# Last image of a four-layer convolution network: six pieces of the output stage loaded ahead, into the tiles of the finished scans

## The chip, the cores and the metric

The kernel runs on one core of a Trainium2 chip. The metric is the device time of one execution in microseconds (us). The core has a tensor engine (TensorE, matmuls, results in PSUM), a vector engine (VectorE), a scalar engine (ScalarE), GpSimd, and SyncE (SP), whose queue issues nearly all DMA transfers here. The engines run their own instruction streams and wait for each other by semaphores. A profile takes one execution apart.

## The reference

Four layers run one after the other on a tensor of 4 images with 64 channels of 128 x 128. The first three (attention with a spectral gate, Fourier mixing with experts, a Hartley layer with a Gaussian blur) are untouched. The change lies in the last one, which sums two state-space scans and its input:

```python
ys = mamba_fwd(xs, ...)                      # one sequence over all images and pixels
spa = silu(group_norm(ys, gn_w, gn_b, 4)) + x
ye = mamba_fwd(xe, ...)                      # short sequences over groups of channels
spe = x + silu(group_norm(ye, ...))
w = softmax(att_w)
return spa * w[0] + spe * w[1] + x
```

The group norm needs mean and variance of a whole image, so an image's output can only be finished once its scan has ended. Layer 2 masks the columns 33 to 95 of every row to zero, up to the blur's edges, so only 69 (`CW`) or 65 (`KW`) of the 128 columns of x are kept; in the masked columns the output is one constant per channel.

## The kernel before

Layer 3 (`layer3`) splits the work of the scans into units. The last 76 units (19, `SPC`, for each image) belong to the spatial scan: 483 positions each, 170 in an image's last one. A unit has 8 steps, one for each `q` in `ORDER` (0, 2, 4, 6, 1, 3, 5, 7). A step q makes `dA` on ScalarE (`do_exp`, L1472), `dB` on VectorE or GpSimd (`do_dB`, L1488), scans `h` from both on VectorE (`do_scan`, L1493), and multiplies `h` by C on GpSimd (`do_hc`, L1520). TensorE sums the products (`do_sums`); then come `do_y` (L1545) and `spa_out`, which brings the result to SBUF and stores it to the array `y1` in HBM (L1564). The states are eight tiles `hs` (h0 to h7, L1267) and eight tiles `dBs` (dB0 to dB7, L1279), each of 128 partitions x 1024 numbers. Both live to the end of the kernel.

When an image's last unit is through, `affine` (L1688) forms scale and shift of the two norms (`bn_aggr` on VectorE, small matmuls, a square root on ScalarE) and fills the constant columns of the output tiles (L1726). Then `combine` makes the image in eight pieces; piece i holds the rows 8i to 8i+7 in partitions 0 to 63 and the rows 64+8i to 64+8i+7 in partitions 64 to 127. Its parts are:

- part 0: six loads on SP's queue, three for each half of the partitions: f from `y1` (L1747), x from `x2s` (L1748), e from `ye` (L1749), of 138, 138 and 130 KB;
- part 1: SiLU with the norm's scale and shift on ScalarE, of f (L1752) and of e (L1753);
- parts 2 and 4: for half a piece each, the weighted sum of x, f and e as four matmuls with scaled unit matrices into PSUM (`ps_m`, two buffers);
- parts 3 and 5: VectorE copies the sum into the output tile (L1765, two copies for each half), and part 5 issues two stores of 256 KB (L1768).

`parts` gives the tiles f, x, e and out of a piece. They lie one behind the other in one of two buffers `big2`, so piece i shares its buffer with pieces i-2 and i+2, and piece i's loads wait until piece i-2 has been computed.

The order of the instructions on TensorE, VectorE, ScalarE and GpSimd is written out by hand: `scans` gives each call a due time in steps and emits the calls sorted by it. SP's queue is not in that list: the framework's scheduler orders it, and it moves DMAs that are free to go ahead of others. Each DMA on that queue uses one of eight semaphores in turn, and so also waits for the eighth DMA before it. For the first three images the pieces are spread between the units of the next image; for the last image there is nothing after them.

Of the kernel before, what the change touches and what calls it, by code (L numbers as in the profile page):

```python
# [17 lines left out]
NB, C, N = 4, 64, 128  # L18
# [6 lines left out]
ZC = 33  # L25
# [286 lines left out]
class Net:  # L312
# [1303 lines left out]
    def scans(self, us):  # L1616
        nc = self.nc
        self.turn, self.o1s = 0, {}
        chunks = GPX // CPX

        todo = []
        steps = [(u, q) for u in us for q in ORDER]
        by_pool = lambda j: ORDER[j % 8] not in BY_DVE
        for ci, u in enumerate(us):
            do = lambda when, f, *a: todo.append((8 * ci + when, len(todo), f, a))
            spa = u["spa"]
            if spa:
                do(-22.0, self.spa_load, u)
            else:
                for part, when in enumerate((-2.9, 4.7, 6.42)):  # L1630
                    do(when, self.do_first, u, part)
                m, i = divmod(u["at"], 4)
                do(-13.0, self.spe_taps, u)
                for g in range(8 if i == 0 else 0):

                    do(-48.0 + 3 * g if m > 1 else -48.0, self.spe_load, m, g)
                for g in range(8 if i == 3 or u["at"] == chunks - 1 else 0):
                    do(12.3 + 3 * g, self.spe_store, m, g)
            do(-12.9, self.do_x, u)
            for part, when in enumerate((-11.65, -11.25, -10.65, -10.05, -9.8, -9.55, -9.3, -9.0, -8.05)):  # L1640
                do(when, self.do_dt, u, part)
            do(-7.7, self.do_put, u, "dt")
            do(-7.4, self.do_put, u, "dx")
            for k, when in enumerate((-9.07, -8.85, -7.24, -6.59)):
                do(when, self.do_bc, u, k)
                do(when + 0.59, self.do_keep, u, k)
            for i, when in enumerate((4.7, 4.74, 5.9, 9.42, 9.74) if u["kind"] != "run" else ()):
                do(when, self.do_sums, u, i)
            if u["kind"] != "run":
                do(10.76, self.do_y, u)  # L1650
                do(12.2, self.spa_out if spa else self.spe_out, u)
                do(13.64, self.do_stats, u)
        mine = [j for j in range(len(steps)) if not by_pool(j)]
        for j, (u, q) in enumerate(steps):
            do = lambda when, f, *a: todo.append((j + when, len(todo), f, a))
            do(-6.0, self.do_copy, u, q, "dt")
            do(-1.56, self.do_exp, u, q, 0)
            do(-1.2, self.do_exp, u, q, 1)
            if by_pool(j):
                do(-6.5, self.do_copy, u, q, "dx")  # L1660
                do(-4.22, self.do_dB, u, q, nc.gpsimd)
            else:
                do(-1.61, self.do_dB, u, q, nc.vector)
            do(0.1, self.do_scan, u, q, 0)
            do(0.5, self.do_scan, u, q, 1)
            if u["kind"] == "run":
                do(0.55, self.keep_run, u, q)
            else:
                do(0.77, self.do_hc, u, q)
        for k, j in enumerate(mine):  # L1670

            when = mine[k - 1] - 1.28 if k else -2.0
            todo.append((when, len(todo), self.do_sel, steps[j]))
        for ci, u in enumerate(us):
            if u["kind"] == "spa" and u["at"][1] == SPC - 1:
                b = u["at"][0]
                do = lambda when, f, *a: todo.append((8 * ci + when, len(todo), f, a))
                do(15.8, self.affine, b)
                for i in range(8):

                    for part, when in enumerate((4.0, 10.37, 16.3, 16.75, 16.8, 17.51)):
                        do(when + 8 * (i + 1), self.combine, b, i, part)
        E = mybir.EngineType
        with self.tc.manual_schedule(engines={E.PE, E.DVE, E.Activation, E.Pool}):
            for _, _, f, a in sorted(todo, key=lambda x: x[:2]):
                f(*a)

    def affine(self, b):  # L1688

        nc, c3, sm = self.nc, self.c3, self.small  # L1690
        mv = sm.tile([128, 2], F32, name="mv0")
        nc.vector.bn_aggr(mv, self.st0.rearrange("p k s -> p (k s)"))
        s0, t0 = self.norm_affine(sm, mv, c3["gm16w"], c3["spa_gn_w"], c3["spa_gn_b"], self.eps)
        mv = sm.tile([128, 4, 2], F32, name="mv1")
        for g in range(4):
            nc.vector.bn_aggr(mv[:, g, :], self.st1[:, g].rearrange("p k s -> p (k s)"))
        gm = c3["gme"][:, 128 * b : 128 * b + 128]
        four = lambda name: sm.tile([128, 4], F32, name=name)
        p = self.ps("m")
        self.mm(p[:, 0:4], gm, mv[:, :, 0])  # L1700
        mean, q, rs = four("mean4"), four("q4"), four("rs4")
        nc.vector.tensor_copy(mean, p[:, 0:4])
        nc.vector.tensor_tensor(q, mv[:, :, 0], mean, ALU.subtract)
        nc.vector.tensor_tensor(q, q, q, ALU.mult)
        nc.vector.tensor_tensor(q, q, mv[:, :, 1], ALU.add)
        p = self.ps("m")
        self.mm(p[:, 0:4], gm, q)
        nc.scalar.activation(rs, p[:, 0:4], AF.Sqrt, bias=self.eps)
        nc.vector.reciprocal(rs, rs)
        one = lambda name: sm.tile([128, 1], F32, name=name)  # L1710
        s1, t1, m = one("s1"), one("t1"), one("m1")
        for of, to in ((rs, s1), (mean, m)):
            nc.vector.tensor_tensor(of, of, c3["goh"], ALU.mult)
            nc.vector.tensor_reduce(to, of, AX.X, ALU.add)
        nc.vector.tensor_tensor(s1, s1, c3["spe_gn_w"], ALU.mult)
        nc.vector.tensor_tensor(m, m, s1, ALU.mult)
        nc.vector.tensor_tensor(t1, c3["spe_gn_b"], m, ALU.subtract)
        self.st = (s0, t0, s1, t1)

        k0, k1 = one("k0"), one("k1")  # L1720
        nc.scalar.activation(k0, t0, AF.Silu)
        nc.scalar.activation(k1, t1, AF.Silu)
        nc.vector.tensor_tensor(k0, k0, c3["att"][:, 0:1], ALU.mult)
        nc.vector.scalar_tensor_tensor(k1, k1, c3["att"][:, 1:2], k0, ALU.mult, ALU.add)
        for i in range(2):
            nc.vector.tensor_copy(self.parts(i)[3][:, :, ZC:96], k1.unsqueeze(2).to_broadcast([128, 8, 96 - ZC]))  # L1726

    def parts(self, i):

        ws, at, out = (CW, CW, KW, N), 0, []  # L1730
        for w in ws:
            out.append(self.big2[i % 2][:, at : at + 8 * w].rearrange("p (h w) -> p h w", h=8))
            at += 8 * w
        return out

    def combine(self, b, i, part):

        nc, c3 = self.nc, self.c3
        R = 8
        f, x, e, out = self.parts(i)  # L1740
        flat = lambda t: t.rearrange("p h w -> p (h w)")
        sides = ((0, 0, 0, ZC), (ZC, ZC + 4, 96, KW - ZC))
        if part == 0:
            for hh in range(2):
                rows = slice(64 * hh, 64 * hh + 64)
# [8 lines left out]
        elif part in (2, 4):  # L1754
            p = self.three = self.ps("m")[:, : 4 * CW]
            at = slice(2 * part - 4, 2 * part)
            self.mm(p, c3["by_x"], flat(x[:, at]), stop=False)
            self.mm(p, c3["by_0"], flat(f[:, at]), start=False, stop=False)
            p = p.rearrange("p (h w) -> p h w", h=4)
            for j, (of, mid, to, w) in enumerate(sides):  # L1760
                self.mm(p[:, :, mid : mid + w], c3["by_1"], e[:, at, of : of + w], False, j == 1)
        else:
            p = self.three.rearrange("p (h w) -> p h w", h=4)
# [35 lines left out]
```

## Time and profile before

| | us |
|---|---|
| time, median of 3 runs | 7353.47 (7347.41 to 7354.81) |
| profiled execution | 7342.41 |
| its span | 7340.7 |
| last y store issued (L1564) | 7277.78 |
| norms known, first SiLU of the last image's output | 7287.74 |
| first store of its piece 0 / piece 4 | 7293.59 / 7318.42 |
| last copy of piece 7 (L1765) | 7335.34 |

Times in the lower rows are from the span's start. In the profile, lines name engine, line of the kernel, tile, and counts; "A" is a tile in one of the buffers `big2` (or a load tile of the scans), `h` and `dB` are the scans' tiles. A wait line names the waiting instruction, then what it waited for. In the chain of work that ended last, a line "DMA A<-ye" is the time from a load's issue until it has landed, and SPq is SP's queue.

### The profile page before, as it was taken

Reading aid. Unit: us, or ns where it says so; the run is one execution under the profiler, and the core shown is the slowest. Engines: PE = TensorE matmul, PEld = TensorE weight load, DVE = VectorE, ACT = ScalarE, POOL = GpSimd, SP = SyncE. Lnnn points to the kernel's source line nnn. Section 1 sums busy time; section 2 is a strip of 40 time slices with the busy share of each in tenths; the row PEclk is TensorE's granted clock in tenths of the full one; section 3 lists DMA queues with packets and bytes.
Section 4 is the critical chain, followed back from the end, with each engine's and each line's share of the span. In section 5 each row is a group of like instructions: output and inputs, shape, how many; then the busy total and the mean of one; then the engine's idle time right before and its main releaser. Section 6 shows DMA issues by size and latency. Waiting matters only on the chain.

```text
span 7340.7 us, 106844 instructions
## 1 busy us (share of the span) xinstructions
PE 6632.5 (90%) x39058; PEld 2873.7 (39%) x39058; DVE 5408.6 (74%) x7737; ACT 4771.6 (65%) x7768; POOL 3607.2 (49%) x1908
## 2 busy tenths in 40 slices
PE   8998999989999899988899999999899888888897
PEld 6335553347335553346422223222322332332333
DVE  3665546563565546663599999999999899899896
ACT  2564636553564536652588888888788787887885
POOL 1000000000000000000399999999999899899896
PEclk9998989989999989987899999999999999999998
DMA  3000010002000110002455555555454464564554
GB/s 90 1 1 1 28 47 1 1 1 74 1 1 1 28 47 1 1 1 106 133 145 150 149 147 150 149 149 148 133 149 146 129 183 142 143 172 137 156 162 119
DMA packets 364110, 647.03 MB, mean 88 GB/s; under 512 B 46784, under 2 KB 219584, under 8 KB 362048
## 3 DMA queue, kind: packets, MB, share of 16 engines
q1 hardware_dynamic: 357680, 609.91, 30.0%
q10 hardware_dynamic: 5904, 30.28, 1.2%
q8 instruction: 308, 5.05, 0.3%
q14 instruction: 218, 1.79, 0.1%
HBM read 517.80 MB, written 122.22 MB: 87 GB/s over the span
## 4 chain that ended last, share of the span: by engine, by line
PE 48%; DVE 19%; issue 10%; POOL 10%; ACT 8%; DMA 4%; SPq 1%; POOLq 0%; DVEq 0%; ACTq 0%
PE ps_sp L330 14%; DVE h L1493 9%; PE ps_s L330 8%; PE ps_m L330 7%; POOL hc L1520 6%; PE ps_o L330 6%; PE ps_pt L330 4%; DVE dB L1488 3%; POOL dB L1488 2%; PE ps_dx L330 2%; PE ps_y L330 2%; DMA s_dx<-ddx 2%; ACT dA L1472 2%; DVE big L1061 2%; PE ps_m L811 1%
## 5 line engine op out<-in xcount | busy, mean ns | idle before, releaser
L1520 POOL TENSOR_TENSOR hc<-h,C 128x966 f32<-128x966 f32 (+3 forms) x1128 | 2437.4, 2240 | 118.7 <-DVE h L1493 93.2
L1493 DVE TENSOR_TENSOR_SCAN h<-dA,h,dB 128x483 f32<-128x483 f32 (+1 forms) x1200 | 1348.4, 1166 | 54.5 <-ACT dA L1472 54.5
L755 DVE TENSOR_REDUCE nmz<-ps_sp 128x1 f32<-128x320 f32 x2048 | 895.8, 485 | 622.5 <-PE ps_sp L330 613.2
L771 ACT ACTIVATE big<-ps_sp 128x512 f32<-128x512 f32 (+1 forms) x1536 | 830.6, 592 | 720.3 <-PE ps_sp L330 719.0
L1493 DVE TENSOR_TENSOR_SCAN h<-dA,dB 128x512 f32<-128x512 f32 (+2 forms) x1072 | 1222.0, 1190 | 4.0 <-ACT dA L1472 3.9
L930 POOL TENSOR_TENSOR aw<-pack_a 128x128 f32<-128x128 f32 x8 | 3.5, 456 | 2189.8 <-PE ps_m L330 2189.8
L1488 POOL TENSOR_TENSOR dB<-s_dx,B 128x1024 f32<-128x1024 f32 (+5 forms) x450 | 993.7, 2210 | 15.4 <-DMA s_dx<-ddx 6.7
L330 PE MATMUL ps_sp<-uT,kT 32*128 32x512 f32 x3072 | 924.2, 649 | 1.4 <-ACT big L771 0.8
L330 PE MATMUL ps_dx<-dtx,c_sel 128*128 128x483 f32 (+3 forms) x1420 | 754.5, 613 | 188.0 <-DVE dB L1488 186.5
L1488 DVE TENSOR_TENSOR dB<-ps_dx,B 128x1024 f32<-128x1024 f32 (+5 forms) x750 | 810.9, 1083 | 147.4 <-PE ps_dx L330 146.5
L1472 ACT ACTIVATE dA<-s_dt,c_spa_a 128x483 f32<-128x483 f32 (+3 forms) x1232 | 760.8, 640 | 179.0 <-DVE h L1493 176.9
L330 PE MATMUL ps_sp<-kT,qT 32*128 32x320 f32 x4096 | 817.3, 499 | 3.9 <-ACT qT L736 3.3
L1472 ACT ACTIVATE dA<-s_dt,c_spe_a 128x448 f32<-128x448 f32 x1040 | 635.7, 632 | 155.0 <-DVE h L1493 154.2
L330 PE MATMUL ps_y<-hc,c_sum 128*32 128x483 f32 (+3 forms) x4512 | 680.1, 560 | 60.9 <-POOL hc L1520 54.3
L330 PEld LDWEIGHTS ps_dx<-dtx,c_sel 128*128 128x128 f32 x1420 | 225.8, 190 | 661.9 <-DVE dB L1488 225.4
L330 PEld LDWEIGHTS ps_sp<-uT,kT 32*128 32x128 f32 x3072 | 278.8, 185 | 438.3 <-issue 243.0
L330 PE MATMUL ps_o<-big,va 128*32 128x512 f32 (+1 forms) x3072 | 415.6, 613 | 0.0
L330 PE MATMUL ps_s<-pack_a,big 128*64 128x128 f32 (+4 forms) x2832 | 371.0, 307 | 45.6 <-DMA big<-in_x 19.6
L330 PEld LDWEIGHTS ps_sp<-kT,qT 32*128 32x128 f32 x4096 | 358.2, 190 | 57.2 <-issue 36.6
L330 PEld LDWEIGHTS ps_s<-pack_a,big 128*128 128x128 f32 (+2 forms) x2832 | 329.1, 180 | 67.5 <-issue 25.7
L330 PEld LDWEIGHTS ps_y<-hc,c_sum 128*32 128x32 f32 x4512 | 124.9, 109 | 509.4 <-issue 306.8
L454 POOL MEMSET big<- 64x128 f32 x4 | 0.8, 200 | 627.5 <-PE ps_s L330 420.0
(391 smaller groups left out, 10376.4 us busy)
## 6 DMA issues: line engine op xcount, KB each, us to landing
s_dt<-ddt SPq DMA_DIRECT2D x520, 256.0 KB
s_dt<-ddt SPq DMA_DIRECT2D x544, 241.5 KB
s_dx<-ddx SPq DMA_DIRECT2D x195, 256.0 KB
s_dx<-ddx SPq DMA_DIRECT2D x204, 241.5 KB
ddt<-dt SPq DMA_DIRECT2D x65, 256.0 KB
ddx<-dtx SPq DMA_DIRECT2D x65, 256.0 KB
A<-x2s SPq DMA_DIRECT2D x136, 121.2 KB
ddt<-dt SPq DMA_DIRECT2D x68, 241.5 KB
```

The costliest lines, as they stand in the source:

```text
L330: self.nc.tensor.matmul(out, lhsT, rhs, start=start, stop=stop)
L454: nc.gpsimd.memset(mag[64:128, 32, :], 0.0)
L755: nc.vector.tensor_reduce(self.nmz[n % 2][:, j, at : at + 1], p[:, :KEYS], AX.X, ALU.max, negate=True)
L771: nc.scalar.activation(slot(m, 2 * wu + q)[rows], p[rows], AF.Exp)
L811: nc.tensor.transpose(p[:, 128 * j : 128 * j + 128], o[:, 128 * j : 128 * j + 128], k("ident"))
L930: nc.gpsimd.tensor_tensor(aw[i], k(f"aw{i + 1}"), k("sg"), ALU.mult)
L1061: nc.vector.scalar_tensor_tensor(acc(i), y, gate[:, p : p + 1], acc(i), ALU.mult, ALU.add)
L1472: self.nc.scalar.activation(t(u["dA", q][sg][:, u["lo"] : u["n"]]), t(u["dt", q]), AF.Exp, scale=a)
L1488: eng.tensor_tensor(v(dB[:, :, x:y]), v(d), v(u["BC"][0][:, :, x:y]), ALU.mult)
L1493: self.nc.vector.tensor_tensor_scan(h[:, lo:n], u["dA", q][sg][:, lo:n], self.dBs[q][:, sg, lo:n], init, ALU.mult, ALU.add)
L1520: self.nc.gpsimd.tensor_tensor(v(hc), v(self.hs[q][:, :, at]), v(u["BC"][1][:, :, at]), ALU.mult)
```

## The change

For the last image the pieces 2 to 5 get tiles of their own: f, x, e and out of piece 2 are h0 to h3, those of piece 3 are h4 to h7, those of pieces 4 and 5 are dB0 to dB3 and dB4 to dB7. Pieces 0 and 1 keep the two buffers, and pieces 6 and 7 use these again. The loads of the pieces 0 to 5 of the last image have the due times 12.5 to 13.0 after the last unit's start, where before each piece's loads had their due time 8 steps after the previous piece's. `affine` fills the constant columns of six output tiles for the last image.

```diff
-                        do(when + 8 * (i + 1), self.combine, b, i, part)
+                        when += 8 * (i + 1)
+                        if part == 0 and b == NB - 1 and i < 6:
+
+                            when = 12.5 + 0.1 * i
+                        do(when, self.combine, b, i, part)
...
-        for i in range(2):
-            nc.vector.tensor_copy(self.parts(i)[3][:, :, ZC:96], k1.unsqueeze(2).to_broadcast([128, 8, 96 - ZC]))
+        for i in range(2 if b < NB - 1 else 6):
+            nc.vector.tensor_copy(self.parts(b, i)[3][:, :, ZC:96], k1.unsqueeze(2).to_broadcast([128, 8, 96 - ZC]))
 
-    def parts(self, i):
+    def parts(self, b, i):
 
         ws, at, out = (CW, CW, KW, N), 0, []
+        rows = lambda t: t.rearrange("p (h w) -> p h w", h=8)
+        if b == NB - 1 and 2 <= i < 6:
+            flat = [t.rearrange("p s x -> p (s x)") for t in self.hs + self.dBs]
+            return [rows(flat[4 * (i - 2) + j][:, : 8 * w]) for j, w in enumerate(ws)]
         for w in ws:
-            out.append(self.big2[i % 2][:, at : at + 8 * w].rearrange("p (h w) -> p h w", h=8))
+            out.append(rows(self.big2[i % 2][:, at : at + 8 * w]))
             at += 8 * w
         return out
...
-        f, x, e, out = self.parts(i)
+        f, x, e, out = self.parts(b, i)
```

## The prediction

> **What bounds the kernel now.** I read the table of the span in slices first, and then only its end, because the diff is guarded by the last image: everything up to the last unit of the scans is built from the same instructions in the same order on every engine. So I took the stretches of the end, one by one, for engines and DMA.
>
> ```profile
> 7278.00:7288.00 10.00, 3.39 (x10) 2.43 (x10) 5.71 (x26) 3.32 (x7) 0.00 (x0) 0.50 0.02 4
> 7288.00:7297.00 9.00, 7.17 (x30) 5.84 (x30) 2.94 (x11) 2.73 (x4) 0.00 (x0) 0.76 0.37 94
> 7297.00:7305.00 8.00, 5.11 (x14) 4.16 (x15) 0.49 (x2) 1.67 (x2) 0.00 (x0) 0.64 0.83 233
> 7313.00:7319.00 6.00, 4.38 (x16) 3.56 (x16) 0.98 (x4) 1.75 (x3) 0.00 (x0) 0.72 0.77 226
> ```
>
> After the span come busy times of TensorE, its weight loads, VectorE, ScalarE and GpSimd, then the granted clock, the DMA share and GB/s. For 10 us (the two norms, 7278 to 7288) the DMA engines stand still (0.02). From 7297 on they are 0.77 to 0.83 busy and no compute engine is full. The waits from 7288 on say who waits for whom (us in total, times, longest):
>
> ```profile
> DVE A L1765 <- PE ps_m L330: 32.3, 15, 7.1
> ACT A L1752 <- DMA A<-y: 31.1, 6, 8.5
> PE ps_m L330 <- DMA A<-x2s: 14.6, 5, 4.6
> ```
>
> ScalarE waits for a transfer six times, once for each of pieces 2 to 7. Pieces 0 and 1 were loaded long before (their last load was issued at 7130.8). The chain that ended last shows how two pieces take turns:
>
> ```profile
> 7318.42 0.49 SPq L1768
> 7318.95 0.60 SPq L1768
> ...
> 7323.14 3.06 DMA A<-ye
> ...
> 7329.38 2.84 DMA A<-ye
> ...
> 7332.33 0.83 ACT A L1753
> 7333.20 2.12 PE ps_m L330 x12
> 7335.34 0.30 DVE A L1765
> ```
>
> At 7318.42 SP issues the two stores of piece 4. Behind them in its queue stand the six loads of piece 6, the stores of piece 5, the six loads of piece 7; the last of these lands at 7332.22, and 8.5 us later (7340.7) the span ends: norm, matmuls, copy, store. The six pieces that wait take from 7296.3 (piece 1 copied out) to 7335.6, 6.6 us each. What a piece costs when its data is there is seen on TensorE in pieces 0 and 1:
>
> ```profile
> 7292.87 0.63 PE L330 MATMUL ps_m<-A,c_by_x 128*128 128x276 f32 x2
> 7293.34 1.08 PE L330 MATMUL ps_m<-A,c_by 128*128 128x276 f32 x6
> 7294.26 0.62 PE L330 MATMUL ps_m<-A,c_by_x 128*128 128x276 f32 x2
> ```
>
> Half a piece every 1.39 us (7292.87 to 7294.26), so 2.78 us a piece; ScalarE needs 1.46 (its four starts 7287.74, 7288.48, 7289.19, 7289.93) and VectorE 2 x 0.49.
>
> **The change part by part.** *Loads of pieces 2 to 5 moved.* 24 DMAs: 4 x (2 x 138 + 2 x 138 + 2 x 130 KB) = 3.3 MB. As built, they stand on SP's queue from the last but one s_dt load of the last unit on, and have these waits. The first, into dB0, waits for VectorE's scan of the unit's first step (over at about 7261.9). Behind it is the last s_dt load; its own wait is ScalarE's exponentials of the third step, which already wait for that same scan because dA has two steps of buffers. So it is late by one issue, 0.6 us. Before, it was issued by 7262.88, which with the 2.84 us of a landing gives 7265.7, and ScalarE reads it in the group at 7270.81: 5 us of cover; without that, 0.6 us on the scans' chain. The next loads wait for GpSimd's hc of steps 1 to 3 (over by 7268.5); behind them is the y store of the last but one unit, whose source is ready at 7270.91: no delay. The next wait for hc of step 7 (about 7274.05); behind them is the last y store, ready at 7277.75: none either, and piece 7 alone reads it. After it, 13 loads are left: 13 x 0.64 us (the pitch of 7301.39, 7302.03, 7302.66) = 8.3 us, so issued by 7286.7 and landed by 7289.6. Piece 5 is wanted on ScalarE at about 7293.6. 4 us of cover, in a stretch whose DMA share was 0.02; cost nothing. SP itself is next wanted at 7293.57, for piece 0's store.
>
> *Four more fills of the constant columns (L1726).* 0.42 us each, but two take 0.76, so a pitch of 0.34: four more are 1.36 us of VectorE, from 7289.05 to 7290.4. TensorE's first half piece ends at 7290.8, and the copy waits for that. Cost nothing; uncovered 1.4.
>
> *Pieces 2 to 5 computed without waiting.* They follow pieces 0 and 1 at 2.78 us each. Piece 1 was copied out at 7296.33, so pieces 2, 3, 4, 5 are at 7299.1, 7301.9, 7304.7, 7307.4. Piece 4's stores go out at 7304.7 instead of 7318.42: **13.7 us earlier**. Here the clock matters. The trace grants 0.50 in 7300 to 7306, after TensorE had idled 4.09 us: piece 2 took 5.8 us. The Trainium skill (TensorE: Matmul & The Clock Gate, What's actually happening) has the clock halved after an idle window of about 3.4 us. Pieces 2 to 5 now have no such gap; at the half clock each would take 5.8, four of them 12 us more. But the rule also speaks against the change: after piece 5 TensorE idles some 4 us until piece 6's data is in, so piece 6 may run at the half clock (5.8 instead of 2.8). Before, piece 6 was already half cold (7325.78 to 7330.62) and still ended ahead of piece 7's landing; if the cold lasts into piece 7, half a piece more is 1.5 us at the end. I keep that for the range.
>
> *The two last loads.* The queue as built is: stores of 0 to 4, loads of 6, stores of 5, loads of 7, stores of 6 and 7. So from piece 4's stores on the same 16 DMAs are issued as before. Before, that took 7318.42 to 7329.97 = 11.55 us: the first eight 5.41 (pitch 0.68, the same as from 7306.20 to 7311.60), the last eight 6.14 (0.77, with two issues of 1.02 and 1.18 us). At 0.68 throughout it is 10.8. I put the slow issues down to a DMA backlog: piece 5's loads were landing until 7319.8, when piece 4's stores were already issued. In the changed kernel only piece 3's stores are then in flight. So 10.8 (and 11.55 as the other end), 2.25 from there to landing, and 8.5 to the end, of which piece 7's first half took 2.0 against 1.54 at full clock: 8.0 to 8.5.
>
> The transfers allow it. Stores of 2 x 0.52 MB and loads of 2 x 0.83 MB are 2.71 MB; between 7308 and 7318 the five windows of 2 us moved 249, 240, 240, 245 and 235 GB/s: 11.2 us, and landing is 13.0 after the first issue. The Trainium skill (SBUF — State Buffer, Door 1: The DMA port swizzle) gives a transfer over partitions 0 to 63 only half the ports, about 218 GB/s; then 12.4 us, and with about 1 us to the first byte 13.4. That is 0.4 later; the 242 GB/s measured here for the same 64-partition pieces decide. During pieces 2 to 4 the stores ask 0.52 MB in 2.78 us = 189 GB/s, and the last two stores alone moved in 2.1 us (250), so they don't pile up.
>
> **Sum.** 7304.7 + 10.8 + 2.25 + 8.0 = 7325.7 for the end of the span, 15.0 under 7340.7; with the slow pitch and 8.5 at the end it is 7327.0, 13.7 under. I take 15.0, as the backlog that goes with the slow pitch is gone. The profiled execution took 7342.41, 1.7 more than its span, and the runs' median is 11.1 above it; the difference of 15.0 is carried over: 7353.47 - 15.0 = **7338.5 us**. 0.2% is 14.7 us, about what a measurement of this kernel can tell from no change, so the forecast stands almost on that line.
>
> **The rivals.** *The tail stays slow (0.13):* cold clock in pieces 6 and 7 (1.5 to 4 us) or the loads landing 2 to 5 us later under the stores. For it: the clock fell to 0.5 in three of the six waits. Against: piece 6 ends under piece 7's transfer. Gain 5 to 12, so 7341 to 7348, within 0.2%.
>
> *Only the bytes bind (0.05):* after 7293.6 there are 8 x 0.52 + 2 x 0.83 = 5.9 MB, 24.2 us at 242, so with the end of the last store about 7321: gain 20, 7333. Against: the order on SP puts piece 7's loads behind piece 5's stores.
>
> *The transfer was not the limit (0.04):* if something else sets the pace of 6.6 us a piece, nothing moves: 7353. Against: no compute engine is full, and pieces 0 and 1 ran at 2.78.
>
> *Slower (0.06):* the last s_dt load, now behind a load that waits for VectorE, lands too late. Its exponentials, scan, hc and sums hang on it, and so does the norm. It has 5 us of cover, and the tail gains 15: beyond 20 us of lateness it costs more than the change brings, and at 35 the time is 7368. Against: the wait in front of it ends before its own.
>
> **How the numbers follow.** The likeliest case has 0.72, its own range 7336 to 7342; seven parts in ten of it lie beyond 14.7, because the backlog is gone. Faster by over 0.2%: 0.72 x 0.72 + 0.05 = 0.57. Within: 0.20 + 0.13 + 0.04 = 0.37. Slower 0.06. The runs before scatter over 7.4 us. The range for 8 in 10 is 7333 to 7346: the bytes alone below, most of the slow tails above.
>
> **What would show it.** The stretch 7278 to 7288 has a DMA share of 0.3 or more; ScalarE waits for y in two pieces instead of six; TensorE runs from 7288.6 to 7307 without a gap, clock 1.0 from 7294; piece 4's stores are issued near 7304.7, and the span ends near 7325.7. It is wrong if a load into h or dB is still waited for, if pieces 6 and 7 take more than 14 us from piece 4's stores to landing, or if the last scan is late.

## The result: 14.35 us by the medians, and the profile after

| | before | after |
|---|---|---|
| time, median of 20 runs each | 7352.86 (7339.41 to 7359.77) | 7338.51 (7329.55 to 7344.25) |
| ratio | | 0.9982, 95% interval 0.9976 to 0.9988 |
| profiled execution / its span | 7342.41 / 7340.7 | 7330.85 / 7328.6 |
| last y store issued | 7277.78 | 7276.31 |
| first SiLU of the last image's output | 7287.74 | 7286.27 |
| first store of piece 4 | 7318.42 | 7303.82 |
| tail: from that SiLU to the end of the span | 52.96 | 42.33 |

The ratio alone makes 13.2 us of 7352.86, its interval 8.8 to 17.6. The line of 0.2% (14.7 us), on which the forecast almost stood, lies inside it. The profiled execution reached the tail 1.47 us earlier. Where the scans end differs by more than that between two executions of one kernel (below), so from here on I compare tails and not spans.

The stretches of the end, in the columns of the prediction:

```profile
7278.00:7288.00 10.00, 3.67 (x10) 2.56 (x11) 6.43 (x29) 3.74 (x8) 0.00 (x0) 0.50 0.65 180
7288.00:7297.00 9.00, 9.00 (x41) 7.70 (x41) 3.36 (x13) 7.06 (x10) 0.00 (x0) 0.76 0.27 69
7297.00:7305.00 8.00, 8.00 (x49) 7.01 (x48) 2.78 (x12) 0.00 (x0) 0.00 (x0) 1.00 0.73 188
7305.00:7311.00 6.00, 1.03 (x7) 0.75 (x5) 0.67 (x3) 0.52 (x1) 0.00 (x0) 0.86 0.88 238
7311.00:7316.00 5.00, 4.81 (x13) 3.85 (x14) 0.49 (x2) 1.15 (x2) 0.00 (x0) 0.50 0.68 198
```

The 10 us of the norms, in which the DMA engines stood still (0.02), now carry loads (0.65). From 7288 to 7305 TensorE is busy without a gap, at the full clock from 7297 at the latest. Then it idles for more than 5 us and goes on at the half clock. In the kernel after, the loads have the lines L1756 to L1758, the SiLUs L1761 and L1762, the copies L1774 and the stores L1777; in the experiments these shift by a few. The waits from 7288 on (us in total, times, longest):

```profile
DVE A L1774 <- PE ps_m L330: 19.9, 8, 7.7
ACT A L1761 <- DMA A<-y: 19.9, 2, 15.4
PE ps_m L330 <- DMA A<-x2s: 6.5, 2, 5.2
```

ScalarE waits for a transfer for two pieces where it waited for six. Those two are 6 and 7, and it still stands 19.9 us for them. TensorE, which is busy until 7306, feels 6.5 us of that. The chain that ended last shows the same two steps:

```profile
7287.16 16.12 PE ps_m L330 x78
7303.30 0.50 DVE dB L1774 x2
7303.82 0.47 SPq L1777
...
7308.58 3.05 DMA A<-ye
...
7313.56 2.16 SPq L1757
7315.77 2.75 DMA A<-ye
...
7319.50 3.78 PE ps_m L330 x12
7323.31 0.30 DVE A L1774
```

First 16.12 us of nothing but matmuls, then the stores of piece 4, and behind them on SP's queue the loads of pieces 6 and 7. Two entries are longer than before: one DMA issue of 2.16 us, and piece 7's last matmuls with 3.78 where it was 2.12.

### The profile page after: what moved, and what is told of

It is laid out like the page before. It is cut to its first block, busy times and chain, and to the rows that moved or that the text cites. A ratio compares the mean times of both kernels' runs of the same rounds, so it can differ in the third digit from the quotient of the medians.

```text
span 7328.6 us, 106826 instructions
## 1 busy us (share of the span) xinstructions
PE 6624.9 (90%) x39058; PEld 2869.6 (39%) x39058; DVE 5407.1 (74%) x7741; ACT 4774.0 (65%) x7768; POOL 3608.6 (49%) x1908
## 4 chain that ended last, share of the span: by engine, by line
PE 49%; DVE 16%; POOL 10%; issue 10%; ACT 8%; DMA 5%; SPq 1%; POOLq 0%; DVEq 0%; ACTq 0%
PE ps_sp L330 14%; PE ps_m L330 9%; DVE h L1493 7%; PE ps_s L330 7%; POOL hc L1520 7%; PE ps_o L330 6%; PE ps_pt L330 4%; PE ps_dx L330 3%; DVE dB L1488 3%; PE ps_y L330 3%; DMA s_dx<-ddx 2%; POOL dB L1488 2%; ACT dA L1472 2%; DVE big L1061 2%; DMA big<-in_sr 2%
```

## The experiments

Every row gives the tail, from the first SiLU of the last image's output to the end of the span, in one profiled execution. Where the scans end varies by many microseconds between executions (the last y store is issued at 7276.31 in the changed kernel's first profile, at 7283.41 in its second, at 7291.30 in e4's), so spans can't be compared, and tails can. All medians are of 6 to 20 runs, each ratio is to the kernel before on the same chip. They stem from three sessions, in which the kernel before had medians of 7352.86 (row "after"), 7349.36 (e1, e3, e4, e5) and 7348.66 ("after, again", e6, e8); so between sessions only ratios are compared, and the intervals, 9 to 17 us wide, are large beside most differences.

| kernel | tail | pieces 4 and 7 copied out, after the first SiLU | median | ratio, 95% |
|---|---|---|---|---|
| before | 52.96 | 30.65, 48.09 | 7352.86 | |
| before, again | 54.34 | 32.13, 49.41 | | |
| after | 42.33 | 17.52, 37.53 | 7338.51 | 0.9982 (0.9976 to 0.9988) |
| after, again | 38.64 | 16.82, 33.87 | 7335.82 | 0.9984 (0.9975 to 0.9994) |
| e1: two pieces ahead | 44.07 | 22.29, 39.22 | 7341.38 | 0.9991 (0.9984 to 0.9998) |
| e3: loads of 6 and 7 early | 31.98 | 17.68, 25.97 | 7326.20 | 0.9974 (0.9964 to 0.9983) |
| e4: all eight ahead | 29.94 | 16.80, 25.09 | 7326.16 | 0.9972 (0.9963 to 0.9981) |
| e5: TensorE kept busy | 40.62 | 17.50, 35.79 | 7336.87 | 0.9981 (0.9974 to 0.9987) |
| e6: instructions shifted | 38.30 | 16.56, 33.53 | 7338.01 | 0.9988 (0.9979 to 0.9998) |
| e8: e4 and a warm-up | 29.69 | 16.60, 24.89 | 7326.81 | 0.9971 (0.9960 to 0.9983) |

**Half the dose.** Only pieces 2 and 3 get tiles of their own; 4 to 7 take turns in the two buffers.

```diff
-                        if part == 0 and b == NB - 1 and i < 6:
+                        if part == 0 and b == NB - 1 and i < 4:
...
-        for i in range(2 if b < NB - 1 else 6):
+        for i in range(2 if b < NB - 1 else 4):
...
-        if b == NB - 1 and 2 <= i < 6:
+        if b == NB - 1 and 2 <= i < 4:
```

> Only pieces 2 and 3 get the h tiles and are loaded ahead; pieces 4 to 7 share the two buffers as before. I measure the tail: from the first SiLU of the last image's output to the end of the span, 52.96 us in the profile before (7287.74 to 7340.7) and 42.33 in the profile after (7286.27 to 7328.6). Theory (each piece loaded ahead saves its turn of store, load and landing; the queue order behind it stays): piece 2's stores go out 12.0 us after the first SiLU, as after, and from there it takes the 34.5 us of before: tail 46.5, so 6.5 us under before, half of the change's gain. Rival (only the bytes bind): 8 x 0.52 + 4 x 0.83 = 7.5 MB at 242 GB/s are 31 us, tail 38. Rival (the transfers are not the limit): tail 53.

Measured: a tail of 44.07, 8.9 under before. That is less than the 46.5 that the theory gave, and far from the values of both rivals. On SP's queue four of the six loads of piece 4 now stand behind the stores of piece 2:

```profile
7290.38 1.11 SPq L1777 DMA_DIRECT2D out<-h  x2
7291.59 0.55 SPq L1758 DMA_DIRECT2D A<-ye  x1
...
7301.75 1.13 SPq L1777 DMA_DIRECT2D out<-A  x2
```

Piece 4 goes out at 22.29, after pieces 0 to 3 at 5.39, 8.16, 10.92 and 13.68. Half of the pieces loaded ahead bring half of the gain or more (8.9 of the 10.6 to 14.3 in the tails, 6.6 of 13.2 by the ratios), so it is the loading ahead that pays. Of the 2.4 us by which the tail is shorter than expected, 1.05 lie ahead of piece 2's stores, where TensorE left the half clock earlier (3.80 us after the first SiLU, 6.02 in the kernel after); the rest has the size of the scatter between two executions of one kernel, shown below.

**The order on SP's queue, with the same bytes and tiles.** Only the due times of the last two pieces' loads change: they stand behind the stores of pieces 0 and 1, whose buffers they use, and no longer behind those of pieces 4 and 5.

```diff
                             when = 12.5 + 0.1 * i
+                        if part == 0 and b == NB - 1 and i >= 6:
+                            when = 25.6 + 8 * (i - 6)
```

> As the changed kernel, but the loads of piece 6 stand on SP's queue right behind the stores of piece 0, those of piece 7 right behind the stores of piece 1 (before: behind the stores of pieces 4 and 5). No tile and no byte differs. Theory (the order on SP's queue is what holds pieces 6 and 7 back): TensorE never waits after piece 0, piece 7 is copied out 25.8 us after the first SiLU, tail 31 to 33, some 10 us under the changed kernel. Rival (the bytes bind, at 218 GB/s for 64 partitions): 5.9 MB from the first store on, 26.9 us, tail 35. Rival (latency of stores and loads as such): tail stays at 42.

Measured: 31.98, as the theory gave. SP's queue, and then two stretches:

```profile
7293.82 1.13 SPq L1779 DMA_DIRECT2D out<-A  x2
7295.06 0.53 SPq L1758 DMA_DIRECT2D A<-y  x1
...
7299.21 1.18 SPq L1779 DMA_DIRECT2D out<-A  x2
...
7304.23 0.59 SPq L1760 DMA_DIRECT2D A<-ye  x1
```

```profile
7300.00:7304.00 4.00, 4.00 (x25) 3.52 (x24) 1.48 (x6) 1.67 (x2) 0.00 (x0) 1.00 0.83 244
7308.00:7312.00 4.00, 4.00 (x25) 3.52 (x24) 1.37 (x6) 0.24 (x1) 0.00 (x0) 1.00 0.87 289
```

The last load is issued at 7304.23, 16.7 us after the first SiLU, where the changed kernel issues it 29.5 after (7315.77). TensorE runs through all eight pieces (4.00 of 4.00 at clock 1.00) while the DMA engines move 244 GB/s (loads and stores) and then 289 GB/s (stores alone, as the last loads have landed) beside it; the rival's 218 GB/s, taken over from the prediction, did not bind. In the changed kernel it is thus the place of the last twelve loads on the queue that holds back pieces 6 and 7, and not the amount to be moved. This is shown by the profile: tiles and bytes are the same, and only the order on the queue differs. It is worth 10.3 or 6.7 us in the tails (against the two profiles of the changed kernel), which is beyond their scatter of 3.7. By the ratios it is about 6 us, but the intervals of e3 and of the kernel after overlap, so the runs of e3 alone would not show it; e4 and e8 point the same way.

**All eight ahead.** Pieces 6 and 7 too get tiles that the scans have finished with: four of `hc`, two each of B and C.

```diff
...
-                        if part == 0 and b == NB - 1 and i < 6:
+                        if part == 0 and b == NB - 1:
...
-        for i in range(2 if b < NB - 1 else 6):
+        for i in range(2 if b < NB - 1 else 8):
...
+        if b == NB - 1 and i >= 6:
+            if i not in self.more:
+                names = ("hc",) * 4 if i == 6 else ("B", "B", "C", "C")
+                self.more[i] = [self.work.tile([128, 2, 512], F32, name=k, bufs=6 if k == "hc" else 2) for k in names]
+            flat = [t.rearrange("p s x -> p (s x)") for t in self.more[i]]
+            return [rows(t[:, : 8 * w]) for t, w in zip(flat, ws)]
```

> Pieces 6 and 7 also get tiles of their own, from the buffers of hc, B and C that the scans no longer use, and are loaded ahead too: after the first store there is nothing but stores. Theory (order on SP): the same as with the early loads, tail 31, as TensorE's 2.78 us a piece sets the end in both. If the bytes bind in the run with early loads, this one is shorter by that much: only 4.2 MB are left, 17 us. A price could come from the 12 more loads on SP's queue between the last unit's small transfers and piece 0's stores: they are issued by about 5.5 us after the first SiLU, the first store is due 6.3 after it, so none is expected.

Measured: 29.94.

```profile
7305.87 0.59 SPq L1764 DMA_DIRECT2D C<-ye  x1
7307.04 3.87 SPq L1783 DMA_DIRECT2D out<-A  x4
...
7326.38 1.11 SPq L1783 DMA_DIRECT2D out<-C  x2
```

All loads are issued before the first store, and TensorE makes up the tail: 5.75 us until piece 0 is copied out, seven pieces at 2.76, and 4.85 behind the last copy. The median is that of e3 in the same session (7326.16 and 7326.20): once TensorE is the limit, still earlier loads bring no gain that the runs show. The tail is 2.0 us shorter than e3's. Of these, 1.2 lie behind the last copy: from there to the end it is 4.8 to 4.9 us in all profiles but e3's, where it is 6.0; there the DMA engines are still busy with the stores of earlier pieces. By the ratios they beat the kernel after by some 6 and 7 us.

**The half clock in pieces 6 and 7.** Seven unread matmuls keep TensorE busy while it waits for pieces 6 and 7.

```diff
+                        if part == 4 and b == NB - 1 and i in (5, 6):
+                            do(when + 0.05, self.keep_warm, 4 if i == 5 else 3)
...
+    def keep_warm(self, n):
+        for i in range(n):
+            self.mm(self.dA[i], self.c3["id"], self.c3["sel"][:, :512])
```

> The changed kernel with seven extra matmuls that nobody reads: four after piece 5 and three after piece 6, to keep TensorE busy while it waits for loads. Theory (the half clock in piece 7 is part of the end: 3.78 us where 2.12 were seen at full clock): clock near 1.0 in pieces 6 and 7, tail 42.3 - 1.6 = 40.7. Rival (landing alone sets the end, or the extra matmuls run into piece 7's own): tail 42 or more.

Measured: 40.62, and the chain ends with piece 7 at the full clock. Piece 6 was not kept at it, as had been expected: its second half ran at 0.50 (7316.62 to 7320.03).

```profile
7316.34 3.70 PE ps_m L330 x12
7320.04 2.64 PE dA L330 x6
7322.68 2.78 PE ps_m L330 x16
```

Piece 7 takes 2.78 us, where the same 16 matmuls took from 7318.01 to 7323.31, 5.3 us, in the first profile of the kernel after; there a wait for the SiLU of e is in it, and the last twelve took 3.78 where 2.12 were seen at the full clock. But the unread matmuls themselves (2.64) stand in front of it on the chain, and the runs show no gain over the kernel after (0.9981 and 0.9982). The tail of 40.62 fits the forecast; as the next run reaches 38.64 with no edit at all, it proves nothing by itself.

**Both kernels once more.** No edit.

> The kernel before, unchanged: a second look, for how much the tail (first SiLU of the last image's output to the end of the span) differs between two executions of one program. The first look had 52.96 us. Theory: nothing in the tail is random except the phase of TensorE's clock, so within 2 us of 52.96. If it is off by more, single tails can't carry the comparison.

> The changed kernel, unchanged: a second look. The first had a tail of 42.33 us, with 2.16 us for one DMA issue among piece 7's loads and piece 7's matmuls at half clock (3.78 us). Theory: both are parts of this program and come back: tail 41 to 43.5. Rival (chance of one execution): the issue takes 0.6 us or the matmuls 2.1 us, tail 39 to 41.

Before: 54.34, within 2 us as expected. After: 38.64, 3.7 less than in the first profile. My theory, that 41 to 43.5 belongs to this kernel, fell: the 42.33 was partly chance, as the rival had it, and the new value lies even below the rival's 39. SP's queue in this second profile:

```profile
7310.21 1.11 SPq L1777 DMA_DIRECT2D out<-dB  x2
...
7319.22 0.59 SPq L1756 DMA_DIRECT2D A<-y  x1
7319.86 0.59 SPq L1757 DMA_DIRECT2D A<-x2s  x1
7320.50 0.60 SPq L1758 DMA_DIRECT2D A<-ye  x1
```

The issue that took 2.16 us takes 0.59 here. The 3.69 us between the two profiles are 0.70 up to piece 4's stores (17.55 and 16.85 after the first SiLU), 1.57 from there to the landing that the chain waits for (14.70 and 13.13), and 1.42 from there to the end (10.08 and 8.66). The 0.70 fit the clock: the half clock lasted until 6.02 us after the first SiLU in the first profile and 4.57 in the second, and 1.45 us more of it are 0.7 us of matmuls lost.

**What the long issue goes with.** In the first profile's stretch from 7313 to 7316.5 the DMA queues hold one packet that is no data:

```profile
q8 instruction: 1, 0.02, 2.9%
```

That is a fetch of instructions, on a queue of its own (q8). To move it, 40 one-column matmuls, whose results nothing reads, are put on TensorE before the scans.

```diff
+        todo.append((-21.0, len(todo), self.filler, (40,)))
...
+    def filler(self, n):
+        p = self.ps("m")
+        for i in range(n):
+            self.mm(p[:, i : i + 1], self.c3["id"], self.c3["one"])
```

> The changed kernel with 40 one-column matmuls that nobody reads, issued by TensorE before the first unit of the scans. They move every later instruction of TensorE by 40 matmuls within its instruction stream, and change nothing at the end of the kernel. In the three looks in which an issue among piece 7's loads took 1.18 to 2.16 us, a packet of the instruction queue q8 was moved in the same 2 to 3 us; in the run with two pieces ahead it came after these loads, and no issue there took over 0.95. Theory (the instruction fetch stalls the loads): the fetch falls elsewhere, no issue among piece 7's loads takes more than 1.1 us, and the tail is 1 to 1.6 us shorter, 41. Rival (the issues wait because the transfers are behind): the issue of 2 us comes back at the same load, wherever the fetch falls. The 40 matmuls themselves cost up to 10 us at the start of the scans.

Measured: 38.30, no issue over 0.97 us among the loads of piece 7, and no fetch among them. Across all profiles, an issue of 1.04 to 2.16 us among the last four of piece 7's loads and a fetch at the same time occur together four times (before, before again, after, e5), and neither occurs there in the three others that have this part of the queue (e1, after again, e6). But the unedited kernel lost its long issue as well, so this run does not separate the cause from chance. The whole profiles say more. In the first one of the kernel after, 118 of the 2931 DMA issues on SP have a fetch of 16 KB running in their first half microsecond, and 23 of these take over 1 us; of the other 2813, 10 do. The other nine profiles are alike: 18 to 26 of 104 to 124, against 6 to 14 of some 2810. So the long issues go with the fetches all through the kernel. That the fetch is the cause is likely, but no run isolates it, and most issues beside a fetch are not long.

**The cold first piece.** e4, with six unread matmuls of 256 columns spread over the two norms, so that piece 0 need not start at the half clock.

```diff
+        self.warm()
...
+        self.warm()
...
+    def warm(self):
+        for i in range(3 if self.last else 0):
+            self.mm(self.dA[i][:, :256], self.c3["id"], self.c3["sel"][:, :256])
```

> All eight pieces loaded ahead, and six extra matmuls of 256 columns that nobody reads, three after the second and three after the fourth small matmul of the norms, to have TensorE at full clock when piece 0 starts. Theory: piece 0 is copied out 3.4 to 4.5 us after the first SiLU instead of 5.75 to 6.3, and the tail is 28 to 29 instead of 29.94; the time is that much under the run with all eight ahead. Rival (the extra matmuls delay the norms' small ones, or are too few to change the clock): tail 30, and the norms (last y store to first SiLU, 9.96 us in both looks) take longer.

Measured: 29.69, no better than e4 beyond scatter. Piece 0 still runs at the half clock:

```profile
7296.25 1.13 PE L330 MATMUL ps_m<-A,c_by_x 128*128 128x276 f32 x2
7297.17 1.98 PE L330 MATMUL ps_m<-A,c_by 128*128 128x276 f32 x6
7298.96 0.66 PE L330 MATMUL ps_m<-A,c_by_x 128*128 128x276 f32 x2
```

1.13 and 1.98 us for what takes 0.62 and 1.08 at full clock. The norms take 9.96 us as before, so the rival's second half (the unread matmuls are too few) is what happened. They filled 2.91 us of about 5 twice, and even a stretch in which TensorE was busy for 2.99 of 3.41 us was followed by the half clock (third from the end):

```profile
7288.76:7292.17 3.41, 2.99 (x8) 1.85 (x7) 2.69 (x8) 0.00 (x0) 0.00 (x0) 0.50 0.81 217
7292.17:7295.59 3.42, 2.48 (x8) 2.13 (x8) 1.80 (x13) 1.83 (x5) 0.00 (x0) 0.50 0.81 223
```

## Why the prediction came out right, step by step

The forecast's tail is 7325.7 - 7287.74 = 37.96 us. The two profiles of the changed kernel have 42.33 and 38.64, the means of two profiles each (53.65 and 40.49) differ by 13.2, and the ratio says 13.2 too. The forecast was 15.0. Its mechanism is borne out: pieces 2 to 5 no longer wait, and 6 and 7, which still do, are held by the order on SP's queue. That the median of 7338.51 meets the forecast of 7338.5 is luck: the sums below are 0.7 and 4.4 us off, and the ratio leaves 8.8 to 17.6 us open. The terms:

| step | predicted | after | after, again |
|---|---|---|---|
| first SiLU to piece 4's stores | 16.96 | 17.55 | 16.85 |
| piece 4's stores to the landing that the chain waits for | 13.05 | 14.70 | 13.13 |
| landing to the end | 7.95 | 10.08 | 8.66 |
| sum | 37.96 | 42.33 | 38.64 |

In the second profile the chain goes through piece 7's x and not through its last load, e, which had landed by 7323.73, when ScalarE read it:

```profile
7319.86 3.48 DMA A<-x2s
```

*Loads moved at no cost: right.* The first moved load and the last s_dt load behind it on SP's queue, and then ScalarE's group that reads it:

```profile
7258.94 0.47 SPq L1756 DMA_DIRECT2D dB<-y  x1
7259.51 0.55 SPq L1462 DMA_DIRECT2D s_dt<-ddt  x1
```

```profile
7270.13 1.38 ACT L1472 ACTIVATE dA<-s_dt,c_spa_a 128x170 f32<-128x170 f32 x4
```

From issue to use are 10.6 us; with the 2.84 of a landing 7.8 are left, where I had counted 5. ScalarE waits for no s_dt load there, and the rival on the slower side did not happen. The last of the moved loads is issued at 7284.49, before the first SiLU, and of pieces 2 to 5 none is waited for. Whether the new tiles alone bring this order on SP's queue or the new due times are needed too, no run separates.

*Four more fills: right.* The six end at 7288.90, and the first copy waits for TensorE until 7289.35.

*Pieces 2 to 5: right.* They are copied out at 12.00, 14.76, 17.52 and 20.29 after the first SiLU, 2.76 apart.

*The last two loads: right in size, wrong in its reason.* In the first profile these DMAs are issued in 12.55 us (7303.82 to 7316.37), even more than the 11.55 of before; in the second 10.89, and in e6 11.06, against the 10.8 that I took. My reason was that a backlog of transfers makes issues slow, and that it would be gone. That reason is not borne out: the long issue began when the DMA engines were 0.86 busy (7313 to 7314), but it hung on until 7315.72, when they had run dry (0.10 busy with 24 GB/s in 7315 to 7316), so a backlog does not explain its length. The sign that I had named for being wrong (more than 14 us to landing) appeared in the first profile and not in the second.

*The end, 8.0: too small in both profiles.* The smaller part is a misreading. The 8.5 of before were taken to hold half a microsecond of half clock in piece 7's first half (2.0 against 1.54). But the clock was full there; those matmuls waited for the SiLU of e (1.00 is the granted clock, third from the end):

```profile
7331.90:7335.40 3.50, 3.27 (x16) 2.38 (x16) 0.55 (x3) 0.99 (x2) 0.00 (x0) 1.00 0.57 150
```

So there was nothing to save: after the second profile's landing piece 7 ran at the full clock too, and yet it took 8.66 (8.3 from 7323.73, when e had surely landed).

The larger part, in the first profile alone, is the assumption that piece 7 runs at the full clock. There the granted clock changed at 7309.36 (to 0.50), 7316.18 (to 1.00), 7319.60 (to 0.50) and 7323.01 (to 1.00), which is 6.83, 3.41 and 3.41 us apart. That agrees with the Trainium skill (TensorE: Matmul & The Clock Gate, What's actually happening), which has the clock judged over free-running windows of 3.4 us. The stretches between these changes show what such a window held (first TensorE's busy time, then its granted clock):

```profile
7312.77:7316.18 3.41, 3.41 (x12) 2.79 (x11) 0.49 (x2) 0.00 (x0) 0.00 (x0) 0.50 0.53 153
7316.18:7319.60 3.42, 1.73 (x9) 1.04 (x8) 0.49 (x2) 1.67 (x2) 0.00 (x0) 1.00 0.67 159
```

The same kernel again, where piece 7's data came 0.8 us and not 1.37 us after piece 6's last matmul:

```profile
7321.82:7325.24 3.42, 2.62 (x15) 1.92 (x14) 0.49 (x2) 1.67 (x2) 0.00 (x0) 1.00 0.48 112
```

After the window with 1.73 us of matmuls the clock fell to 0.50 again (7319.60 to 7323.01), and piece 7 paid for it; after the one with 2.62 it stayed at 1.00. In that profile the late last load so counts twice, once as a wait and once as a cold clock. I had counted 1.5 us for the range and nothing in the sum. (That the long issue made the window emptier follows from the order of events in one profile; it was not tried by itself. And 1.73 us are no threshold: see the last section.)

*The rivals.* "Only the bytes bind" would have ended the tail near 7321 on the scale of before. e3 shows that the order on the queue stood before the bytes, and that with another order TensorE binds, with some 1.2 us for the last stores: 7287.74 + 31.98 = 7319.7. "The transfer was not the limit" is out by e1 and by the result. "The tail stays slow" occurred in part, in one profile of two (1.65 and 2.13 us over the terms). Over the two profiles the tail is 2.5 longer than the forecast (4.37 and 0.68) and that of before 0.7 longer than the one it was made against: 15.0 - 2.5 + 0.7 = 13.2.

## What to carry to other kernels

A tail in which loads, compute and stores take turns in two buffers can borrow the memory of whatever has ended before it; here that turned 6.6 us a piece into 2.76. When some pieces no longer wait, look at where the others' loads stand on the queue that issues them: moving twelve issues ahead of stores brought another 6.7 to 10.3 us in the tail without a byte of memory (e3). And a single profile of a tail of 40 us may be off by 4: take a second one of the unchanged kernels before explaining a difference of that size.

## What had not been expected of the hardware

- In these tails a load behind another takes 0.59 us to issue on SP and the pitch is 0.64, but now and then one takes 1.0 to 2.2 us. Issues over 1 us go with fetches of instructions in all ten profiles (23 of 118 against 10 of 2813 in the kernel after). The second load behind a pair of stores takes 0.90 to 1.15 us, with no fetch beside it (0.72 and 0.84 once each in the two profiles of before); why is open.
- The clock fell to 0.50 after windows in which TensorE was not idle: 1.73 us of matmuls in 3.42 in the kernel after, 1.60 in e5. The idle window that the prediction reckoned with was not needed. But the busy time of the profile does not decide it. In the same profile of the kernel after, 45 us before the tail, the clock stayed at 1.00 behind a window with only 1.54 us:

```profile
7241.09:7244.50 3.41, 1.54 (x10) 0.16 (x8) 3.41 (x5) 1.79 (x4) 3.41 (x2) 1.00 0.39 120
7244.50:7247.91 3.41, 2.15 (x8) 0.65 (x12) 3.41 (x5) 1.45 (x3) 3.41 (x3) 1.00 0.19 57
```

In the profile of before it fell behind one with 2.87 of 3.41 us (2674.18 to 2677.59), made of small matmuls. What is counted is open.

- Stores of 64 partitions each, several at a time and for both halves of the partitions, moved 289 GB/s over 4 us in e3. The prediction had weighed 218 (the Trainium skill, SBUF — State Buffer, Door 1: The DMA port swizzle) against the 242 measured for loads and stores together; neither was their limit. The same section puts the partitions 0 to 63 and 64 to 127 on different ports. Whether that is why both halves side by side exceed one half's figure is not shown.
